# First batch's chains of pieces take turns between the attention's steps; last parts fetch operands during the experts of the chunk in front

## The chip, the cores and the metric

The kernel runs on one core of one Trainium2 chip. The metric is the device time of one execution in microseconds (us). A core has a matrix engine (TensorE, PE in the profile; PEld are its weight loads), a vector engine (DVE), an engine for functions such as exp (ACT), a general engine (POOL), and SP, which here only issues DMAs. Each engine takes its instructions strictly in the order in which the program gives them[...].

## The reference

The input x is 4 batches of 64 x 64 tokens with 128 channels, all float32. Two layers follow each other:

- Layer 0: elu(x), a 3x3 convolution 128 to 128, a second one 128 to 256 whose halves a and b give c3 = a * sigmoid(b); then a causal attention over the 4096 tokens of a batch with one query and key of 4 channels and a value of 16 channels, whose result goes through W3; x + c3 + that is the layer's output t.
- Layer 1: t = t + A(layernorm(t)), where A is an attention with 16 heads of 8 channels over all 4096 tokens, followed by its output product wo and a gated FFN of width 344 with a residual each; then t = t + M(layernorm(t)), where M routes each token to 2 of 8 experts (a 128 x 128 product and a bias each) and adds them with their gates.

In layer 1 the attention is the large part: per batch 16 heads x 4096 x 4096 exponentials.

## The kernel before, in words

A batch is cut into 8 chunks of 512 tokens. All work on layer 1's attention is done in **steps** (`attention_step`, line 820): one key tile of 128 tokens against one chunk of 512 queries for 4 heads. A step has four score matmuls on PE (`s<-qx,f_kx`), two exps of 128 x 1024 on ACT (`e<-s`), and four value matmuls on PE (`acc<-e,vg`), which `finish` (line 234) lets run two steps behind the scores. A batch has 8 chunks x 4 groups of 4 heads x 32 key tiles = 1024 steps, the kernel 4096.

`plan` (from line 1146) lists the steps as segments. A batch can only begin when its queries, keys and values exist. So the first batch goes in three turns: with the first 2 chunks alone (n = 2, 64 steps), then with 4 chunks (192 steps), then with all 8 (768 steps); partial sums go to DRAM (`d_p`). The other batches go in one turn of 1024 steps. A segment may start when `second` of its batch, the number of chunks whose operands are ready, has reached n.

Everything else is written as Python generators, "chains", each cut into **pieces** by `yield cost, word`: `convolutions` (line 439, Winograd products `m<-v,f_wino`, their sums on DVE and their row and column terms `r` and `v` on POOL), `first_attention` (line 576, layer 0's attention for a chunk, whose own steps go through `steps_in`), `second_operands` (line 650: product with W3, layernorm, transposition `m<-f_consts,h`, queries, values and keys of layer 1 for a chunk, stored to DRAM), and `last_part` (line 863: everything of a chunk after its attention, up to the output). "held" means that the piece has left its PSUM bank half written; "wait" and "rounds" that it has nothing to do until something else is done.

Before the first step, and after the last one, the chains run without steps (`alone[0]` is True): `run_alone` (line 1044) goes round all of them, and `bank` (line 162) hands out three PSUM buffers in turn. While steps run, `alone[0]` is False, and all chains share **one** PSUM bank, `m`. They stand in the list `fillers`; `insert` (line 245) takes one piece of the first one after a step. How often is set by `credit` and `rate` in the main loop (lines 1241 to 1267): one piece a step while the first batch is not ready, and later so many that the estimated rest is spread over the steps left. `quiet` keeps the first two steps of a segment free of pieces. While `stream` has no step to give, because `second` is too small, the loop counts as `waiting` and inserts one piece per turn.

In the first batch after line 1237 the list holds `second_operands_beside` (line 736), which returns at once when no chunk is ready, and `first_attention`. The latter does everything in one chain: if it lacks the convolution of its chunk it takes a piece of `st.conv` itself (line 583), then does the chunk's layer 0 attention, then runs `second_operands` for it (line 645), then takes the next chunk.

`last_part` loads its operands from DRAM (sums and values of the attention, h and t), stores the reciprocals of the sums, loads them again spread over the heads (`per`), and multiplies; eight pieces with no work on PE give the DMAs time. Further down, the experts' gates are turned by a store to DRAM (`d_g<-turned`) and four loads (`g<-d_g`), six empty pieces follow, then the product of the gates with the experts' biases (`tokens(ps, g8, eb, ...)`), then the experts' own products: for each of 4 token blocks two halves, which DVE multiplies by the gates (`by_e`), sums (`added`) and adds to t; then t is stored.

In the profile nearly all instructions carry line 105, since the class `InOrder` issues them all; groups are told apart by the names of their tiles.

Of the kernel before, what the change touches and what calls it, by code (L numbers as in the profile page):

```python
# [115 lines left out]
def fast_path(ctx: ExitStack, tc: tile.TileContext, a: dict, where: dict, out: bass.AP, verdict):  # L116
# [45 lines left out]
    def bank():  # L162
        return s_tile()[:, :QB] if alone[0] else m_tile()
# [275 lines left out]
    def convolutions(b, st):  # L439
# [88 lines left out]
        for n, (layer, r) in enumerate(jobs):  # L528
            ahead, terms = [], []
            at_once = False  # L530
            if n + 1 < len(jobs):
                layer_, r_next = jobs[n + 1]
                if layer_ == 0:
                    yield from elu(min(2 * r_next + 3, NQ))
                    if r_next == 3:
                        pool.memset(e_band[1][:, 17, :], 0.0)

                at_once = layer_ == 0 or layer == 1 or r_next + 1 < r
                if at_once:
                    terms.append(row_terms((c_band if layer_ else e_band)[r_next % 2]))  # L540

            def used(q):
                if at_once:
                    ahead.append(col_terms(terms[0], COLS[q]))

            if layer == 0:
                yield from winograd(wino1, slice(0, C), v, b1, used, first(r))
                here, above = c_band[r % 2], c_band[(r - 1) % 2]
                if r == 0:
                    pool.memset(here[:, 0, :], 0.0)  # L550
                else:
                    pool.tensor_copy(here[:, 0, :], above[:, 16, :])
                    pool.tensor_copy(above[:, 17, :], here[:, 1, :])
                if r == 3:
                    pool.memset(here[:, 17, :], 0.0)
            else:
                while alone[0] and len(st.ready) < 2 * r - 2:
                    yield 0.0, "wait"
                st.c3 = wk.tile([P, 2 * QB], FP, tag="c3", bufs=2, name="c3")
                yield from winograd(wino2, slice(0, C), v, half_b2a, lambda q: None, second(r, False))  # L560
                yield from winograd(wino2, slice(C, 2 * C), v, b2[:, 1:2], used, second(r, True))
                st.done += [st.c3[:, :QB], st.c3[:, QB:]]
                yield 0.0, "done"
            if n + 1 < len(jobs) and not at_once:
                terms.append(row_terms(c_band[r_next % 2]))
                ahead = [col_terms(terms[0], j) for j in COLS]
            v = ahead
# [8 lines left out]
    def first_attention(b, st):  # L576
        top0 = small("top0", [2, NQ])
        top_v0 = small("topv0", [NQ])
        xt = load_x(b, 0, "xt")
        for c in range(NQ):  # L580
            while len(st.done) <= c:

                yield (0.0, "wait") if alone[0] else next(st.conv, (0.0, "stop"))
            while alone[0] and st.second < c - 1:
                yield 0.0, "wait"
            c3 = st.done[c]
            t = xt
            pool.tensor_tensor(by_k(t), by_k(t), b3.unsqueeze(1).to_broadcast([P, 4, C]), ALU.add)
            if c + 1 < NQ:
                xt = load_x(b, c + 1, "xt")  # L590

            ps = bank()
            yield from halves(ps, wq0, c3)
            u, qx0 = chunk("u"), chunk("qx0")
            dve.tensor_scalar(u, ps, bq0, 0.25, ALU.add, ALU.mult)
            dve.tensor_reduce(top0[:, 0, c : c + 1], u, AX.X, ALU.max, apply_absolute_value=True)
            two_terms(u, qx0, "q")
            yield 0.46, "stop"
            ps = bank()
# [12 lines left out]
            u = chunk("u")[:, :P]  # L612
            dve.tensor_scalar(u, ps[:, :P], bk0, None, ALU.add)
            v0c = v0[:, 4 * c : 4 * c + 4, 1 : 1 + DV0]
            dve.tensor_tensor(
                v0c,
                few[:, :, :DV0],
                bv0.unsqueeze(1).to_broadcast([P, 4, DV0]),
                ALU.add,
            )  # L620
            dve.tensor_reduce(top0[:, 1, c : c + 1], u, AX.X, ALU.max, apply_absolute_value=True)
            dve.tensor_reduce(
                top_v0[:, c : c + 1],
                v0[:, 4 * c : 4 * c + 4, :].rearrange("p k s -> p (k s)"),
                AX.X,
                ALU.max,
                apply_absolute_value=True,
            )
            two_terms(u, kx0[:, c, :], "k")
            yield 0.24, "stop"  # L630

            ps = bank()
            transposed(c3, ps)
            dve.tensor_tensor(t, ps, t, ALU.add)
            yield 0.6, "stop"

            while alone[0] and st.read < c:
                yield 0.0, "wait"
            sums, found = [], []
            for r in range(c + 1):  # L640
                steps_in.append(first_step(c, r, qx0, sums, found))
            while not found:
                yield 0.0, "rounds"
            st.ready.append((t, found[0]))
            while not alone[0] and st.second <= c:
                yield from second_operands(b, st)
        dve.tensor_reduce(seen[:, 0, b : b + 1], top0.rearrange("p i c -> p (i c)"), AX.X, ALU.max)
        dve.tensor_reduce(seen[:, 1, b : b + 1], top_v0, AX.X, ALU.max)
# [87 lines left out]
    def second_operands_beside(b, st):  # L736

        while st.second < NQ:
            while len(st.ready) <= st.second or not folded[0]:
                if not alone[0]:  # L740
                    return
                yield 0.0, "wait"
            yield from second_operands(b, st)

# [75 lines left out]
    def attention_step(b, seg, kt, place, qx, vg, part):  # L820
# [19 lines left out]
        def values(es):  # L840
# [8 lines left out]
            if kt == seg.hi - 1:  # L849
# [5 lines left out]
                to = scratch[b]["a"][c, g] if seg.hi == NT else scratch[b]["p"][g, c]  # L855
                sp.dma_start(out=to, in_=at)
                if seg.hi == NT and g == NG1 - 1:
                    fillers.append([last_part(b, c), LAST])

        return scores, values  # L860


    def last_part(b, c):
        d = scratch[b]
        t, h, an = chunk("xt", "t"), chunk("xe", "h"), chunk("pos", "an")

# [4 lines left out]
        sp.dma_start(out=h, in_=d["h"][c])  # L871
        sp.dma_start(out=t, in_=d["t"][c])
        for _ in range(3):
            yield 0.0, "stop"
        dve.reciprocal(rs, rs)
        sp.dma_start(out=d["r"][c], in_=rs)
        per = chunk("pos", "per")
# [1 line left out]
            out=per, in_=d["r"][c].rearrange("(j i) n -> j (i n)", i=HD1).unsqueeze(1).to_broadcast([NH1, HD1, QB])  # L879
        )  # L880
        for _ in range(4):
            yield 0.0, "stop"
        dve.tensor_tensor(an, an, per, ALU.mult)
        yield 0.0, "stop"
        ps = bank()
        tokens(ps, an, wo1, range(2))
        yield 0.46, "held"
# [97 lines left out]
        by_block = d["g"][c].rearrange("(b e) (k a) -> b e k a", e=SLOT, a=SLOT)  # L985
        for b_ in range(4):
            sp.dma_start(out=g8.rearrange("e (k b a) -> b e k a", k=4, a=SLOT)[b_], in_=by_block[b_, :NE])
        for _ in range(6):
            yield 0.0, "stop"

        ps = bank()
        tokens(ps, g8, eb, range(2))
        yield 0.46, "held"
        tokens(ps, g8, eb, range(2, 4))
        dve.tensor_tensor(t, ps, t, ALU.add)
        yield 0.46, "stop"
        for k in range(4):
            tk = t[:, k * C : (k + 1) * C]
            by_e = wk.tile([P, NE, C], FP, tag="two", bufs=1, name="by_e")
            for half in range(2):  # L1000
# [8 lines left out]
                if half == 1:  # L1009
                    added = chunk("w", "added")[:, :C]  # L1010
                    dve.tensor_reduce(added, by_e.rearrange("p e c -> p c e"), AX.X, ALU.add)
                    dve.tensor_tensor(tk, tk, added, ALU.add)
                yield 0.46, "stop"
        sp.dma_start(out=tb_o[b][:, 4 * c : 4 * c + 4, :], in_=by_k(t))


# [23 lines left out]
            batches.append(self)  # L1040

    batches = []

    def run_alone(gens, until):

# [189 lines left out]
        lambda: st.second >= plan[0].n and len(spread_of) == 3,  # L1235
    )
    alone[0] = False

    fillers.extend([gen, PREPARE] for gen in reversed(left[1:]) if gen is not st.conv)

    steps = stream()
    credit, waiting = 0.0, False
    while True:
# [11 lines left out]
        b = now[0]  # L1255
        if batches[b].second == NQ and len(batches) == b + 1 and b + 1 < B:
            Batch(b + 1)
            fillers.append([first_attention(b + 1, batches[b + 1]), PREPARE])

        rate = 1.0  # L1260
        if batches[b].second == NQ:
            within = steps_left[b] - 40 if b + 1 < B else min(steps_left[b] - 40, 160)
            rate = sum(us for _, us in fillers) / max(1, within)
        credit = min(0.7, credit + rate)
        if waiting or credit > 0.0 and not quiet[0]:
            credit -= insert()
        finish(2)
    finish(0)
    alone[0] = True
# [718 lines left out]
```

## Time and profile before

| what | value |
|---|---|
| median of 3 runs | 8251.99 us (8248.94 to 8252.69) |
| profiled execution | 8255.66 us, its span 8253.9 us |
| mean granted PE clock | 0.983 |
| PE busy | 8031.3 us, 97% of the span |
| ACT busy | 7874.2 us, 95% |
| DVE busy | 2468.4 us, 30% |
| POOL busy | 680.1 us, 8% |
| exps of the steps, `e<-s` | 8480 instructions |
| first step of the attention of layer 1 | 149.5 us after the span's start |
| end of the last step's value matmuls | about 8171 us |

The profiled execution's own time is 1.8 us above its span and 3.7 us above the median of the runs. Busy times of PE are modelled, since matmuls overlap each other, so a PE that is busy all the time need not be at its limit. In the views below, a line of the timeline gives start, length, engine, operation, output<-input and count, and in brackets how long the engine was idle before and who ended that. A line of a table by windows gives the stretch, its length, then busy time and number of instructions of PE, PEld, DVE, ACT and POOL, the granted PE clock, the DMA share and GB/s. A line of the chain of waits gives start, length and what the end of the program was waiting for at that time. A line of the waits gives the total, the number and the longest, in us.

### The profile page before, as it was taken

Reading aid. Unit: us, or ns where it says so; the run is one execution under the profiler, and the core shown is the slowest. Engines: PE = TensorE matmul, PEld = TensorE weight load, DVE = VectorE, ACT = ScalarE, POOL = GpSimd, SP = SyncE. Lnnn points to the kernel's source line nnn. Section 1 sums busy time; section 2 is a strip of 40 time slices with the busy share of each in tenths; the row PEclk is TensorE's granted clock in tenths of the full one; section 3 lists DMA queues with packets and bytes.
Section 4 is the critical chain, followed back from the end, with each engine's and each line's share of the span. In section 5 each row is a group of like instructions: output and inputs, shape, how many; then the busy total and the mean of one; then the engine's idle time right before and its main releaser. Section 6 shows DMA issues by size and latency. Waiting matters only on the chain.

```text
span 8253.9 us, 172977 instructions
## 1 busy us (share of the span) xinstructions
PE 8031.3 (97%) x73299; PEld 2481.4 (30%) x73299; DVE 2468.4 (30%) x5068; ACT 7874.2 (95%) x8679; POOL 680.1 (8%) x615
## 2 busy tenths in 40 slices
PE   7799999999999999999999999999999999999997
PEld 3222222223333322333333333233333333332233
DVE  4433222222322223333322222343332222221223
ACT  3599999999999999999999999999999999999996
POOL 2210211000000003110000000311100000000000
PEclk8799999999999999999999999999999999999998
DMA  2121001101100001111100000111111111111211
GB/s 75 52 71 64 27 32 40 52 26 50 48 24 24 30 19 35 35 38 47 39 30 25 27 28 19 33 36 48 35 42 49 44 40 46 52 38 38 66 60 38
DMA packets 213940, 334.24 MB, mean 40 GB/s; under 512 B 31555, under 2 KB 107811, under 8 KB 213155
## 3 DMA queue, kind: packets, MB, share of 16 engines
q1 hardware_dynamic: 209139, 321.31, 11.9%
q8 instruction: 577, 9.45, 0.5%
q10 hardware_dynamic: 4016, 1.77, 0.1%
q14 instruction: 208, 1.70, 0.1%
HBM read 195.09 MB, written 127.93 MB: 39 GB/s over the span
## 4 chain that ended last, share of the span: by engine, by line
PE 87%; issue 7%; DVE 2%; ACT 1%; DMA 1%; POOL 1%; SPq 0%; ACTq 0%; DVEq 0%; POOLq 0%
PE acc L105 42%; PE s L105 29%; PE m L105 17%; ACT e L105 1%; DVE h L105 0%; POOL rs L105 0%; DMA f_kx<-d_k 0%; DVE pos L105 0%; DVE added L105 0%; DMA xe<-in_x_dram 0%; POOL xt L105 0%; DVE at L105 0%; SPq L105 0%; DMA d_r<-sums 0%; DVE two L105 0%
## 5 line engine op out<-in xcount | busy, mean ns | idle before, releaser
L105 ACT ACTIVATE e<-s 128x1024 f32<-128x1024 f32 (+1 forms) x8480 | 7814.2, 1101 | 144.5 <-PE s L105 137.9
L105 PE MATMUL acc<-e,vg 128*9 128x512 f32 x32768 | 4335.4, 595 | 1.0 <-DVE at L105 1.0
L105 PE MATMUL s<-qx,f_kx 32*128 32x512 f32 (+2 forms) x16960 | 2912.0, 496 | 40.3 <-ACT e L105 24.8
L105 PEld LDWEIGHTS s<-qx,f_kx 32*128 32x128 f32 (+1 forms) x16960 | 1165.5, 182 | 4089.1 <-ACT e L105 3872.2
L105 PEld LDWEIGHTS acc<-e,vg 128*9 128x9 f32 x32768 | 719.6, 90 | 798.0 <-issue 458.5
L105 PE MATMUL m<-v,f_wino 128*32 128x256 f32 x5744 | 468.1, 400 | 18.8 <-POOL v L105 7.3
L105 DVE TENSOR_TENSOR by_e<-m,gates 128x512 f32<-128x512 f32 x245 | 169.4, 691 | 681.6 <-PE m L105 681.6
L105 POOL TENSOR_TENSOR v<-r 128x1024 f32<-128x1024 f32 x120 | 232.6, 1945 | 1160.7 <-PE m L105 1160.3
L105 DVE COPY sd<-m 128x512 f32<-128x512 f32 x179 | 123.7, 691 | 633.5 <-PE m L105 633.5
L105 PE MATMUL m<-f_we,y2T 128*32 128x256 f32 x3920 | 313.1, 391 | 0.0
L105 POOL TENSOR_TENSOR rs<-ve,f_minus_half 128x4 f32<-128x4 f32 x64 | 65.3, 1020 | 2843.5 <-DVE ve L105 2819.8
L105 DVE TENSOR_REDUCE added<-by_e 128x128 f32<-128x1024 f32 x128 | 255.7, 1998 | 4.4
L105 DVE TENSOR_TENSOR t<-m,t 128x512 f32<-128x512 f32 x62 | 42.9, 692 | 698.7 <-PE m L105 698.7
L105 POOL TENSOR_TENSOR t<-t,h 128x512 f32<-128x512 f32 x32 | 40.9, 1277 | 2527.4 <-DVE h L105 2527.4
L105 DVE COPY at<-acc 128x512 f32<-128x512 f32 x130 | 89.9, 692 | 521.3 <-PE acc L105 521.3
L105 PE MATMUL m<-hT,f_fw 128*32 128x256 f32 (+1 forms) x2728 | 236.1, 391 | 0.0
L105 DVE TENSOR_TENSOR t<-m,sums 128x256 f32<-128x256 f32 x135 | 57.3, 424 | 480.1 <-PE m L105 480.1
L105 PEld LDWEIGHTS m<-v,f_wino 128*32 128x32 f32 x5744 | 116.4, 109 | 203.5 <-issue 155.0
L105 DVE SCALAR_TENSOR_TENSOR h<-m,h 128x512 f32<-128x512 f32 (+1 forms) x93 | 64.2, 690 | 352.6 <-ACT th L105 254.5
L105 DVE COPY h<-m 128x512 f32<-128x512 f32 (+1 forms) x93 | 64.2, 690 | 314.1 <-PE m L105 314.1
L105 PE MATMUL m<-e,f_v 128*32 128x512 f32 (+2 forms) x1128 | 154.0, 593 | 0.0
L105 DVE TENSOR_TENSOR e<-e,f_consts 128x128 f32<-128x128 f32 x128 | 29.1, 286 | 315.1 <-ACT e L105 315.1
(253 smaller groups left out, 3319.9 us busy)
## 6 DMA issues: line engine op xcount, KB each, us to landing
f_kx<-d_k SPq DMA_DIRECT2D x139, 512.0 KB
qx<-d_q SPq DMA_DIRECT2D x152, 256.0 KB
d_q<-two SPq DMA_DIRECT2D x64, 512.0 KB
d_a<-at SPq DMA_DIRECT2D x128, 256.0 KB
vg<-d_v SPq DMA_DIRECT2D x32, 576.0 KB
d_k<-two SPq DMA_DIRECT2D x32, 512.0 KB
d_v<-vc SPq DMA_DIRECT2D x32, 288.0 KB
xe<-in_x_dram SPq DMA_DIRECT2D x32, 256.0 KB
```

Of the source, the lines that this page charges most:

```text
L105: made = op(*args, **kw)
```

## The change

Two things are changed.

In the first batch the remaining chains are kept apart after line 1237 and put into one filler, `together`. It goes round them: one piece of a chain, then the next chain; it stays with a chain over "held" and "rounds", and passes over one that says "wait". For that the chains of batch 0 wait for each other by `b == 0` instead of `alone[0]`, so `first_attention` neither takes pieces of the convolution itself nor runs `second_operands`; `second_operands_beside` does that throughout. And as long as `second` of batch 0 is below 4, each turn of the main loop that inserts a piece inserts a second one.

In `last_part` the fetching of the operands is moved out into a generator `operands`. While the experts of a chunk run, each of their eight halves also takes one step of the `operands` of the last part that follows in the list, if there is one. The product of gates and biases is moved behind the experts, and the six empty pieces ahead of it are gone.

```diff
@@ convolutions, first_attention @@
-                while alone[0] and len(st.ready) < 2 * r - 2:
+                while b == 0 and len(st.ready) < 2 * r - 2:
...
-                yield (0.0, "wait") if alone[0] else next(st.conv, (0.0, "stop"))
-            while alone[0] and st.second < c - 1:
+                yield (0.0, "wait") if b == 0 else next(st.conv, (0.0, "stop"))
+            while b == 0 and st.second < c - 1:
...
-            while alone[0] and st.read < c:
+            while b == 0 and st.read < c:
...
-            while not alone[0] and st.second <= c:
+            while b > 0 and st.second <= c:
@@ second_operands_beside @@
-                if not alone[0]:
-                    return
@@ attention_step @@
-                    fillers.append([last_part(b, c), LAST])
+                    fillers.append([last_part(b, c), LAST, (b, c)])
@@ last_part @@
+    fetching, fetched = {}, {}
+
+    def operands(b, c):
...
+        dve.tensor_tensor(an, an, per, ALU.mult)
+        fetched[b, c] = t, h, an
+        yield
+
+    def fetch(b, c):
+
+        if (b, c) not in fetching:
+            fetching[b, c] = operands(b, c)
+        return next(fetching[b, c], fetching) is None
+
+    def fetch_following(b, c):
+        keys = [part[2] for part in fillers]
+        at = keys.index((b, c)) + 1
+        if at < len(keys) and keys[at]:
+            fetch(*keys[at])
+
+    def last_part(b, c):
+        d = scratch[b]
+        while fetch(b, c):
             yield 0.0, "stop"
-        dve.tensor_tensor(an, an, per, ALU.mult)
-        yield 0.0, "stop"
+        t, h, an = fetched.pop((b, c))
...
-        for _ in range(6):
-            yield 0.0, "stop"
-
-        ps = bank()
-        tokens(ps, g8, eb, range(2))
-        yield 0.46, "held"
-        tokens(ps, g8, eb, range(2, 4))
-        dve.tensor_tensor(t, ps, t, ALU.add)
-        yield 0.46, "stop"
         for k in range(4):
...
+                fetch_following(b, c)
                 yield 0.46, "stop"
+        ps = bank()
+        tokens(ps, g8, eb, range(2))
+        yield 0.46, "held"
+        tokens(ps, g8, eb, range(2, 4))
+        dve.tensor_tensor(t, ps, t, ALU.add)
+        yield 0.46, "stop"
@@ new @@
+    def together(gens):
+
+        gens = list(gens)
+        while gens:
+            for _ in range(len(gens)):
+                r = next(gens[0], None)
+                while r is not None and r[1] in ("held", "rounds"):
+                    yield r
+                    r = next(gens[0], None)
+                gen = gens.pop(0)
+                if r is not None:
+                    gens.append(gen)
+                    if r[0] > 0.0 or r[1] != "wait":
+                        yield r
+                        break
+                if not gens:
+                    return
+            else:
+                yield 0.0, "stop"
@@ main loop @@
-    fillers.extend([gen, PREPARE] for gen in reversed(left[1:]) if gen is not st.conv)
+    fillers.append([together(left), PREPARE, None])
...
             credit -= insert()
+            if b == 0 and batches[0].second < plan[0].n + 2:
+                insert()
```

More of the change, by code (lines that the diff above doesn't have):

```diff
@@ L857, in values @@
                 if seg.hi == NT and g == NG1 - 1:
-                    fillers.append([last_part(b, c), LAST])
+                    fillers.append([last_part(b, c), LAST, (b, c)])
         return scores, values
-    def last_part(b, c):
+    fetching, fetched = {}, {}
+    def operands(b, c):
         d = scratch[b]
@@ L881, in last_part @@
         for _ in range(4):
+            yield
+        dve.tensor_tensor(an, an, per, ALU.mult)
+        fetched[b, c] = t, h, an
+        yield
+    def fetch(b, c):
[10 more added lines that the diff above has]
+        while fetch(b, c):
             yield 0.0, "stop"
-        dve.tensor_tensor(an, an, per, ALU.mult)
-        yield 0.0, "stop"
+        t, h, an = fetched.pop((b, c))
         ps = bank()
@@ L987, in last_part @@
             sp.dma_start(out=g8.rearrange("e (k b a) -> b e k a", k=4, a=SLOT)[b_], in_=by_block[b_, :NE])
-        for _ in range(6):
-            yield 0.0, "stop"
-        ps = bank()
-        tokens(ps, g8, eb, range(2))
-        yield 0.46, "held"
-        tokens(ps, g8, eb, range(2, 4))
-        dve.tensor_tensor(t, ps, t, ALU.add)
-        yield 0.46, "stop"
         for k in range(4):
@@ L1257, in fast_path @@
             Batch(b + 1)
-            fillers.append([first_attention(b + 1, batches[b + 1]), PREPARE])
+            fillers.append([first_attention(b + 1, batches[b + 1]), PREPARE, None])
         rate = 1.0
@@ L1262, in fast_path @@
             within = steps_left[b] - 40 if b + 1 < B else min(steps_left[b] - 40, 160)
-            rate = sum(us for _, us in fillers) / max(1, within)
+            rate = sum(part[1] for part in fillers) / max(1, within)
         credit = min(0.7, credit + rate)
```

## The prediction, made before the changed kernel was run

> **What bounds the kernel now.** I began with the busy times and the forty slices of the page, to see where the two full engines are not full.
>
> ```profile
> PE 8031.3 (97%) x73299; PEld 2481.4 (30%) x73299; DVE 2468.4 (30%) x5068; ACT 7874.2 (95%) x8679; POOL 680.1 (8%) x615
> ...
> PE   7799999999999999999999999999999999999997
> ...
> ACT  3599999999999999999999999999999999999996
> ```
>
> ACT is full but for the first two slices and the last: exps set the pace, and only the two ends have anything to give. Next the busy times by window, cut at the turns of the first batch and at the last step:
>
> ```profile
> 149.50:273.60 124.10, 123.10 (x1148) 36.91 (x1152) 42.52 (x73) 118.54 (x129) 34.59 (x27) 0.95 0.15 44
> 273.60:374.50 100.90, 58.83 (x488) 22.17 (x480) 55.45 (x125) 13.13 (x16) 13.40 (x11) 0.55 0.21 71
> 374.50:795.70 421.20, 406.84 (x3744) 124.47 (x3746) 144.55 (x320) 402.26 (x440) 48.01 (x42) 0.97 0.17 57
> 795.70:815.70 20.00, 4.16 (x32) 2.12 (x26) 7.76 (x18) 1.85 (x4) 0.00 (x0) 0.60 0.64 201
> ...
> 8171.00:8178.40 7.40, 2.72 (x12) 2.06 (x12) 6.92 (x8) 0.00 (x0) 0.00 (x0) 0.83 0.09 35
> 8178.40:8254.00 75.60, 29.93 (x115) 23.32 (x115) 32.28 (x73) 2.12 (x4) 2.42 (x3) 0.61 0.08 24
> ```
>
> Row 1 is the turn with 2 chunks; row 2 the wait for chunks 2 and 3, with ACT busy for 13 us of 101; row 3 the turn with 4 chunks; row 4 the wait for chunk 7. Rows 5 and 6 follow the last step: the rest of chunk 6's experts, then all of chunk 7's last part. The timeline of PE then gives the prices, first a step with one piece, then the same pieces in row 2:
>
> ```profile
> 235.23 0.51 PE L105 MATMUL s<-qx,f_kx 32*128 32x512 f32 x4
> 235.67 0.64 PE L105 MATMUL m<-v,f_wino 128*32 128x256 f32 x8
> 236.12 1.04 PE L105 MATMUL acc<-e,vg 128*9 128x512 f32 x8
> 237.10 0.51 PE L105 MATMUL s<-qx,f_kx 32*128 32x512 f32 x4
> ...
> 277.28 1.87 PE L105 MATMUL m<-v,f_wino 128*32 128x256 f32 x16 [0.96 <-DVE t L105]
> 279.94 1.94 PE L105 MATMUL m<-v,f_wino 128*32 128x256 f32 x16 [0.79 <-DVE sd L105]
> 282.91 1.93 PE L105 MATMUL m<-v,f_wino 128*32 128x256 f32 x16 [1.03 <-DVE t L105]
> ```
>
> From start to start: scores 0.44, piece 0.45, values 0.98, so PE needs 1.42 us for a bare step and 1.87 with one piece. ACT does up to 223 exps per 200 us in its fullest stretches, 1.80 us a step. With one piece PE is just the slower. In the wait two pieces fill the one bank `m`, then DVE must empty it: (285.65 - 277.28)/3 = 2.79 us for each use of the bank. Last, the chain of waits and the waits at the end:
>
> ```profile
> 366.42 3.37 DMA d_k<-two
> 369.85 4.58 DMA f_kx<-d_k
> ...
> 8178.43 0.40 SPq L105
> 8178.91 2.31 DMA sums<-d_a
> ...
> 8220.68 2.23 DMA d_g<-turned
> ...
> 8227.23 5.76 PE s L105 x16
> ```
>
> ```profile
> PE s L105 <- DMA g<-d_g: 11.7, 1, 11.7
> ```
>
> Stored keys need 8 us until the next turn can begin. At the end, chunk 7's first load stands behind chunk 6's output on SP, and PE waits 11.7 us for the turned gates with the experts queued behind.
>
> **What the Trainium skill says.** "Perfetto Trace Analysis", section "Identifying the Most-Contended Engine", says that busy time of matmuls doesn't measure how near PE is to its limit. The trace agrees: PE is shown busy throughout a step that takes 1.87 us, and needs 1.42 of it when no piece is there. "TensorE: Matmul & The Clock Gate", "What's actually happening", says that PE falls to half its clock after a window of little activity. The trace agrees: 16 matmuls on `m` take 1.07 us at 275.25 and 1.94 at 279.94, and row 2 has a granted clock of 0.55. So I price the bank's use in a wait at 2.79 us. "DMA: Bandwidth & Descriptors", "Two DMAs through the same engine are not ordered", says that a DMA which reads what another wrote must be issued only after the first has landed; the trace shows it: `d_g` is issued at 8220.68, the first `g` at 8222.99.
>
> **The change, part by part.** Counts of pieces come from the order in which the two built programs stand.
>
> (1) *Start.* While the first keys load (PE waits until 149.53), the four waiting turns insert eight pieces instead of four. Two more uses of the bank from about 147.1 end near 152.6: **+3**.
>
> (2) *Turn with 2 chunks.* Before: 48 steps with a piece, 16 without: 48 x 1.87 + 16 x 1.80 = 118.6; measured 124.1, so 5.5 go to three slow steps at its start and a POOL wait. After: 37 steps carry two pieces. No double step is in the trace; PE's own work is 1.42 + 2 x 0.45 = 2.33 us. Below that it can't fall, PE being in order. Above: the next piece may only begin when DVE has emptied `m`, which took 0.94 to 1.15 us after the last matmul, and 1.42 us (values and next scores) lie between; so DVE's evacuation is hidden, and if it were not (a POOL or layernorm wait ahead of it), I bound it by +1 us a step. I take 2.33. Further 6 steps have one piece, 21 none, and chunks 2 and 3's seven steps of layer 0 (3 + 4), which before stood in row 2, now run here at 1.80: 37 x 2.33 + 6 x 1.87 + 28 x 1.80 = 147.8, plus the same 5.5, plus 3 for PE waiting at c3's gates (5.1 us before, at 292.7): 156.3 against 124.1, **+32**.
>
> (3) *Wait for chunks 2 and 3.* Before: 100.9. After, the built order has these uses of `m` between the 64th step and the next turn: for chunk 2 transposition, queries, values, keys (354.79 to 365.35 in the trace: 10.6 us), for chunk 3 the two products with W3 (3.7) and the same four (10.6): 24.9. Between them, by turns, 15.5 uses by the convolution for chunks 4 to 7: 15.5 x 2.79 = 43.2. That is the cost of taking turns: nothing in this turn needs them. Before, such pieces lay in steps that ACT bounds. Chunk 3's layernorm holds DVE for 4 (PE waited 4.5 at 354.79), and PE waits 7.3 for row and column terms on POOL (as at 408.66), now with chunk 2's products queued behind. The layernorm's `pow` stands ahead of those terms on POOL; the `vc` memset stands behind them, about when PE gets there: 0 to 2. The keys' 8 us lie beside the last 3.5 uses. Sum 79.4: **-22**.
>
> (4) *Turn with 4 chunks and the wait after it.* Before: 122 steps with a full piece and 96 others (26 of layer 0): 401, measured 421.2 (4 us of slow clock at the start, 10 at 401 to 412, 6 at 476 to 484), then 20.0 of waiting. After: 98 and 120, so 399; slow start 4 again, 6 for gates again, the POOL wait is now in (3). The eighth chunk is ready 44 steps before the turn's end, so row 4 goes. What comes late in its place is batch 1's first load of x, for which exp in `elu` waits on ACT ahead of the steps' exps; at 3117 and 5183 that cost about 4.5. Sum 413.6 against 441.2: **-28**.
>
> (5) *Steps from 815.7 to 8171.* Total pieces in steps stay within 1%, all under ACT. The fetch moves five loads, one store and two DVE operations per chunk earlier on SP and DVE; each gets at least two pieces' time (3.6 us) to land. If SP were held up by one, the next `qx` or `f_kx`, fetched a segment ahead, would still be in time. **0**, from -4 to +4.
>
> (6) *After the last step.* The last part of chunk 7 has none in front of it when it is queued, so its fetch is not early. But the fetches shorten the earlier ones: in the built order chunk 6 ends 38 steps before the last instead of after it. The load `sums<-d_a` then follows the store of `at` (issued at 8171.72) once that has landed, 2.2 (as `d_g`) to 3.4 (as `d_k`) later: 8174.5 instead of 8178.91, **-4.4**. And the experts no longer wait for `g`: DVE can begin at 8220.7 and needs 4 x 3.45 = 13.8 us (8235.7 to 8239.15 is one block), then 0.7 for the biases, whose gates land at 8227: t is complete at 8235.3 instead of 8246.2, **-10.9**. If DVE's cover were gone, PE would wait at the end as it does now.
>
> Sum: 3 + 32 - 22 - 28 + 0 - 15.3 = **-30**. The profiled execution, 8255.7, becomes 8225.4; it stands 3.7 above the median, so I forecast **8222 us**.
>
> **The rivals.** (a) *The first batch gains nothing.* For it: (1) to (3) already sum to +13, and only row 4 pays that back; one further stall a turn, each like the 5 to 9 us seen before, is enough. Against: row 4 goes by 44 steps of margin. Then only (6) remains: about 8237. (b) *The waits are cheaper.* With other chains between, PE's gaps may be too short for the slow clock; a use then costs 1.07 + 0.85 = 1.9 as at 275 to 277, and 26 uses save 0.85 each: 8200. For it: the slowdown came only after 4 us of gaps; against: 1.9 us with 1.07 busy still leaves PE idle for 0.8 of it. (c) *Double pieces choke on the single bank, and the kernel gets slower.* If DVE's evacuation is held behind sums, layernorm or POOL so that each of 37 double steps takes 3.3 us (+37) and each of 26 uses in the wait 3.5 (+19), the time is 8278. It decides from 1.42 us between matmul and empty bank; DVE is busy for 42.5 of 124 us in row 1, and 80 pieces instead of 48 bring that to some 57%, which speaks against. (d) *The change doesn't do what it says*: for chunk 7 the early fetch never happens; that is in (6) already.
>
> **How the numbers follow.** Forecast case 50%, its own range 8207 to 8237 (row (3) at 68 to 88, one stall more or less); (a) 24%; (b) 17%; (c) 9%. About 0.2%, 16.5 us, is what a measurement can tell from no change: faster is below 8235.5. From the forecast case 45 of 50, from (a) 10 of 24, (b) all: faster 0.71; same 0.21; slower 0.08. The range 8198 to 8249 leaves out half of (b)'s lower side, and (c).
>
> **What would show it.** Right: the first step of the 4-chunk turn comes later (near 388), with double steps of 2.33 us before it; ACT no longer idles near 800; from the last step's end to the last output 15 us less; no PE wait for `g`. Wrong: PE waits on DVE or POOL inside double steps; bank uses in the wait far from 2.8 us; exps slowed behind `neg<-xe`; or a changed pace of steps between 1000 and 8000.

## The result, and the profile after

| | before | after |
|---|---|---|
| median of 18 runs each | 8252.22 us (8246.71 to 8257.38) | 8236.88 us (8233.5 to 8242.52) |
| ratio, 95% interval | | 0.9982 (0.9975 to 0.9988) |
| profiled execution | 8255.66 us | 8237.05 us |

The change gains 15 us where 30 were forecast. The size is that of rival (a), but it isn't made up as (a) has it: the first batch loses 15 us, the steps after it gain 18 and the end 16. The page of the changed kernel, busy times and slices of PE and ACT:

```profile
PE 8026.9 (97%) x73335; PEld 2480.2 (30%) x73335; DVE 2459.3 (30%) x5068; ACT 7869.3 (96%) x8679; POOL 680.3 (8%) x615
...
PE   6799999999999999999999999999999999999998
...
ACT  2499999999999999999999999999999999999996
```

Work and its amount are as before. The first two slices of ACT were 3 and 5 tenths full and are now 2 and 4: the first batch got emptier, not fuller. The table by windows of the changed kernel, cut at the same events as the one of before (turn with 2 chunks, wait, turn with 4 chunks, the steps after it, what follows the last step):

```profile
154.90:334.00 179.10, 152.36 (x1504) 48.67 (x1504) 80.95 (x166) 134.68 (x145) 46.85 (x37) 0.97 0.12 37
334.00:417.70 83.70, 47.19 (x440) 17.97 (x432) 47.69 (x88) 0.63 (x1) 30.08 (x24) 0.54 0.21 74
417.70:831.20 413.50, 403.57 (x3532) 122.49 (x3536) 135.48 (x308) 403.17 (x445) 42.62 (x35) 0.98 0.21 68
831.20:8168.50 7337.30, 7295.63 (x67392) 2219.51 (x67384) 2081.29 (x4268) 7313.09 (x8064) 511.40 (x451) 1.00 0.12 38
8168.50:8235.20 66.70, 29.99 (x115) 22.76 (x115) 32.84 (x74) 2.12 (x4) 2.41 (x3) 0.65 0.09 27
```

Against the ledger: the start is at 154.9 instead of 149.5; the turn with 2 chunks takes 179.1 (forecast 156.3, before 124.1); the wait 83.7 (forecast 79.4, before 100.9); the turn with 4 chunks 413.5 with no wait behind it (forecast 413.6, before 441.2); the steps after it 7337 (before 7355, forecast no change); the end 66.7 (before 82.9). Two rows are far off: the turn with 2 chunks, and the steps after the first batch.

What a double step looks like there is in PE's timeline of the changed kernel, first near 162, then where it turns over, then near 211:

```profile
162.27 0.51 PE L105 MATMUL s<-qx,f_kx 32*128 32x512 f32 x4
162.71 1.07 PE L105 MATMUL m<-v,f_wino 128*32 128x256 f32 x16
163.60 1.04 PE L105 MATMUL acc<-e,vg 128*9 128x512 f32 x8
164.57 0.51 PE L105 MATMUL s<-qx,f_kx 32*128 32x512 f32 x4
165.01 1.07 PE L105 MATMUL m<-v,f_wino 128*32 128x256 f32 x16
...
188.27 0.66 PE L105 MATMUL m<-f_consts,pos 128*128 128x128 f32 x4 [1.95 <-DVE pos L105]
192.50 1.08 PE L105 MATMUL m<-v,f_wino 128*32 128x256 f32 x8 [3.58 <-POOL v L105]
...
211.53 0.64 PE L105 MATMUL m<-v,f_wino 128*32 128x256 f32 x8
213.14 0.64 PE L105 MATMUL m<-v,f_wino 128*32 128x256 f32 x8 [0.97 <-DVE t L105]
213.57 1.07 PE L105 MATMUL acc<-e,vg 128*9 128x512 f32 x8
214.56 0.50 PE L105 MATMUL s<-qx,f_kx 32*128 32x512 f32 x4
215.00 0.64 PE L105 MATMUL m<-v,f_wino 128*32 128x256 f32 x8
216.45 0.64 PE L105 MATMUL m<-v,f_wino 128*32 128x256 f32 x8 [0.81 <-DVE sd L105]
```

At 162 the step's two pieces stand in one group of 16 matmuls, both halves of one use of the bank `m`, and the period is 165.01 - 162.71 = 2.30 us: the forecast's 2.33. At 188.27 comes a piece that fills the bank by itself (a transposition), and after it the pairs are shifted by one: at 211.53 the first piece is the second half of one use, the next one the first half of another. Now PE must wait inside the step until DVE has emptied the bank (0.97, 0.81), and the period is 215.00 - 211.53 = 3.47. From the starts of the exps, of the steps in this turn 11 take 2.32 us in the mean and 19 take 3.33; 14 of the 19 stand in three groups between 204.9 and 259.7, and a few of the others wait for something else. Two steps more are slow, for another reason: the step with the transposition takes 9.03 us and the next one 5.18. The second piece of the first needs the terms `v` that POOL is still making (3.58 us of waiting at 192.50), and what stands behind it is slow too (the next eight value matmuls take 1.93 us instead of 1.04). The timeline of ACT shows these steps from the other side, 0.43 us without an exp in a step whose pieces share one use, 7.09 behind the wait for POOL, and 1.53 in a shifted step:

```profile
165.17 1.94 ACT L105 ACTIVATE e<-s 128x1024 f32<-128x1024 f32 x2 [0.43 <-PE s L105]
...
196.11 1.94 ACT L105 ACTIVATE e<-s 128x1024 f32<-128x1024 f32 x2 [7.09 <-PE s L105]
...
215.17 1.94 ACT L105 ACTIVATE e<-s 128x1024 f32<-128x1024 f32 x2 [1.53 <-PE s L105]
```

The end is as predicted. The chain of waits of the changed kernel after the last step:

```profile
8169.19 1.99 DMA d_a<-at
8171.20 2.10 DMA sums<-d_a
...
8212.65 1.51 DMA d_g<-turned
8214.26 1.90 DVE added L105
```

The load of the sums follows the store of `at` directly, and the experts' sums on DVE begin beside the store of the gates; no wait for `g` is left in the chain.

So the theory: a double step costs 2.3 us when its pieces share one use of the bank, and 3.3 when they straddle two; this is what ate the gain of the first batch, and the edits to the last part carry the whole gain. The rivals: two pieces a step are too much for DVE or POOL at that place, however paired; or the gain in the steps after 831 belongs to the turns.

### The profile page after: what moved, and what is told of

It is laid out like the page before. It is cut to its first block, busy times and chain, and to the rows that moved or that the text cites. A ratio compares the mean times of both kernels' runs of the same rounds, so it can differ in the third digit from the quotient of the medians.

```text
span 8235.2 us, 173069 instructions
## 1 busy us (share of the span) xinstructions
PE 8026.9 (97%) x73335; PEld 2480.2 (30%) x73335; DVE 2459.3 (30%) x5068; ACT 7869.3 (96%) x8679; POOL 680.3 (8%) x615
## 4 chain that ended last, share of the span: by engine, by line
PE 88%; issue 7%; DVE 2%; ACT 2%; POOL 1%; DMA 0%; ACTq 0%; SPq 0%; DVEq 0%; POOLq 0%
PE acc L105 42%; PE s L105 29%; PE m L105 18%; ACT e L105 1%; DVE h L105 0%; DVE t L105 0%; POOL rs L105 0%; DVE two L105 0%; DVE sd L105 0%; DVE top L105 0%; POOL xt L105 0%; POOL v L105 0%; DVE at L105 0%; DVE pos L105 0%; POOL r L105 0%
## 5 line engine op out<-in xcount | busy, mean ns | idle before, releaser
L105 ACT ACTIVATE e<-s 128x1024 f32<-128x1024 f32 x8480 | 7813.5, 1113 | 98.1 <-PE s L105 93.9
L105 PE MATMUL s<-qx,f_kx 32*128 32x512 f32 (+1 forms) x16960 | 2910.5, 495 | 38.3 <-ACT e L105 28.3
```

The source lines that it names most:

```text
L105: made = op(*args, **kw)
```

## The experiments

Each kernel was run with several repetitions beside the kernel before, whose own median lay between 8252.2 and 8257.5; each ratio is to the one beside it, and medians of different rows can be compared only to some 5 us. The parts below are cut from each profiled execution by the number of the exp (of 8480): to the first exp of the turn with 4 chunks, that turn with the wait behind it, the steps after it, and what follows the last exp.

| kernel | median, us | ratio to before (95%) | to turn 4 | turn 4 | steps after | end |
|---|---|---|---|---|---|---|
| before | 8252.2 | 1 | 375.5 | 440.2 | 7354.2 | 84.1 |
| the change | 8236.9 | 0.9982 (0.9975 to 0.9988) | 418.6 | 412.5 | 7336.2 | 67.9 |
| last parts alone | 8222.4 | 0.9969 (0.9956 to 0.9981) | 369.2 | 439.9 | 7343.1 | 67.8 |
| turns alone | 8268.4 | 1.0019 (1.0011 to 1.0027) | 417.4 | 412.0 | 7352.3 | 83.5 |
| no second piece | 8253.6 | 1.0002 (0.9993 to 1.0010) | 434.7 | 412.7 | 7336.1 | 67.8 |
| pairs aligned | 8214.8 | 0.9955 (0.9941 to 0.9969) | 394.6 | 414.5 | 7336.0 | 68.0 |
| pairs straddled | 8260.8 | 1.0003 (0.9995 to 1.0012) | 434.6 | 412.9 | 7344.1 | 68.3 |
| biases moved alone | 8228.8 | 0.9970 (0.9959 to 0.9981) | 371.3 | 439.9 | 7347.2 | 68.0 |
| early fetch alone | 8332.3 | 1.0088 (1.0075 to 1.0102) | 373.8 | 437.7 | 7441.5 | 79.0 |
| operands first | 8206.7 | 0.9942 (0.9929 to 0.9956) | 368.8 | 428.4 | 7339.3 | 68.3 |
| operands first, aligned | 8185.3 | 0.9918 (0.9904 to 0.9931) | 349.0 | 427.8 | 7340.8 | 67.6 |
| the same through turn 4 | 8217.0 | 0.9955 (0.9941 to 0.9968) | 363.0 | 449.1 | 7338.0 | 67.0 |

**Halves of the change.** The last parts' edits alone: the first batch's chains as before (`alone[0]` again, no `together`, no second piece).

```diff
-    fillers.append([together(left), PREPARE, None])
+    fillers.extend([gen, PREPARE, None] for gen in reversed(left[1:]) if gen is not st.conv)
...
-            if b == 0 and batches[0].second < plan[0].n + 2:
-                insert()
```

> The early fetch and the moved biases alone; the first batch is treated as in the kernel before. Theory (my ledger with step (5) corrected): the end gives its 16 us (82.9 to 66.8 after the last step), whatever the first batch does, so about 8236 against the 8252 before, and the first batch's turns are worth nothing net. If the 18 us that the steps from 816 to 8171 also lost come from the earlier fetches (fewer stalls at the batches' ends), it is lower than that, 8218 to 8230. Rival: the 18 us come from the turns (chains of batch 1 start at another place): then 8236 exactly and the start and first 816 us as before.

And the turns alone, with `last_part` as before:

```diff
-        while fetch(b, c):
-            yield 0.0, "stop"
-        t, h, an = fetched.pop((b, c))
...
-                fetch_following(b, c)
```

> The first batch's chains by turns and the second piece per step alone; the last parts fetch and add their biases as before. Theory that the first batch as a whole loses: start +5, turn with two chunks +55, wait -17, turn with four chunks -28 and the 20 us wait behind it inside that: +15, so 8267 if nothing in the later steps changes. Rival: the 18 us of the later steps come with the turns: about 8250, no change. The end after the last step stays at about 83 us in both.

Measured: 8222.4 and 8268.4. Beside the 8252.8 of these runs' kernel before, the first gains 30.4 and the second loses 15.6; the sum, -14.8, is the change's -15.3. The halves add up, and the turns are a loss by themselves. Of the 18 us by which the steps after 816 got shorter, 11 come with the last parts' edits and 2 with the turns alone; the other 5 are within what executions differ by (below).

**One piece or two.** The change without the second piece per step.

```diff
-            if b == 0 and batches[0].second < plan[0].n + 2:
-                insert()
```

> The change without the second piece per step (one piece in each step of the turn with two chunks). Theory (double steps are dear because of the one bank): the turn with two chunks falls back from 179 to about 137 us (64 steps at 1.80 to 1.87 and the seven first ones of layer 0), while the wait for chunks 2 and 3 then holds 99 pieces, some 47 uses of the bank at 2.75, so about 130 instead of 84: together +4, 8241. Rival (pieces are dear wherever they stand, but steps hide none of a second piece): the wait grows by less than the turn shrinks, 8215 to 8225.

Measured: 8253.6, 17 us slower than the change, which neither side had expected. Its windows, the turn with 2 chunks and the wait:

```profile
151.90:272.60 120.70, 119.71 (x1136) 35.80 (x1137) 41.86 (x73) 118.53 (x129) 34.49 (x27) 0.97 0.15 45
272.60:434.70 162.10, 97.04 (x840) 35.86 (x838) 89.70 (x183) 13.77 (x18) 45.40 (x35) 0.57 0.14 46
```

The turn shrinks to 120.7 (the seven layer 0 steps, which I had counted here, stay in the wait: 13.77 us on ACT), but the wait, at a granted clock of 0.57, takes 162: 78 us more, where the turn saves 58. Two pieces in a wait cost about 2.8 us, a use of the bank; a straddled pair makes a step only 1.5 us longer (3.33 instead of 1.80). With chains by turns, the second piece is needed.

**How the pair lies.** The second piece only if the first one left the bank half written, and the opposite.

```diff
+        held[0] = r is not None and r[1] == "held"
...
-            if b == 0 and batches[0].second < plan[0].n + 2:
+            if b == 0 and batches[0].second < plan[0].n + 2 and held[0]:
```

> The change, with one condition more: a step takes a second piece only if its first one left the bank half written, so a pair is always both halves of one use of the bank. Theory (parity): a double step that holds one use costs 2.3 us, one that holds the second half of a use and the first half of the next costs 3.4, since PE then waits inside the step for the bank to be emptied. With all 38 double steps aligned the turn with two chunks takes 150 to 160 us instead of 179, with 1 to 5 back in the wait: 8213 to 8222, about 8217. Rival (what costs is the sum of work on VectorE and GpSimd behind two pieces, or the slower clock, not how they pair): the turn stays at 175 or more and the time within 5 us of the change's 8237.

```diff
-            if b == 0 and batches[0].second < plan[0].n + 2:
+            if b == 0 and batches[0].second < plan[0].n + 2 and not held[0]:
```

> The opposite of the aligned pairs: a step takes a second piece only if its first one has closed a use of the bank, so every pair holds the second half of one use and the first half of the next. Theory (parity): the 3.33 us that the change's 19 such steps took now hold for all its double steps, 30 to 38 of them, where the aligned kernel has 24 at 2.30: the turn with two chunks at 180 to 195 us against 178 in the change and 154 with aligned pairs; 8237 to 8255. Rival (what made the 19 steps slow was their place in the turn, for instance what VectorE or GpSimd did then): a turn of about 178 again and no steps at 3.3 before 188 us.

Aligned: 8214.8, 22 us less than the change, all of it before the turn with 4 chunks (394.6 against 418.6; the start differs by 3.6 between these two executions). Windows of that kernel, the turn with 2 chunks and the wait:

```profile
152.20:306.00 153.80, 147.64 (x1472) 49.62 (x1476) 80.11 (x160) 134.33 (x145) 46.10 (x36) 0.97 0.14 44
306.00:394.60 88.60, 50.34 (x476) 19.30 (x468) 49.77 (x94) 0.68 (x3) 30.09 (x24) 0.55 0.20 70
```

These windows run from the first exp of the turn to the end of its last, and on to the next turn's first exp; cut so, the change's turn is 177.8 us and its wait 85.1. So the turn is 24 us shorter, with nearly the same busy time on DVE (80.1 against 80.95), POOL and ACT, and the wait grows by 3. In its PE timeline, at the places where the change had the transposition and where it straddled:

```profile
186.39 0.66 PE L105 MATMUL m<-f_consts,pos 128*128 128x128 f32 x4
...
191.89 1.07 PE L105 MATMUL m<-v,f_wino 128*32 128x256 f32 x16
...
217.27 1.07 PE L105 MATMUL m<-v,f_wino 128*32 128x256 f32 x16
218.16 1.04 PE L105 MATMUL acc<-e,vg 128*9 128x512 f32 x8
219.13 0.51 PE L105 MATMUL s<-qx,f_kx 32*128 32x512 f32 x4
219.57 1.07 PE L105 MATMUL m<-v,f_wino 128*32 128x256 f32 x16
```

219.57 - 217.27 = 2.30; 24 steps of this turn take 2.30, one 3.17. Step by step beside the change, the 24 us have two parts. The 14 steps in three groups that straddled take 33.0 us instead of 47.5: 14.5 less. And the two steps from the transposition on take 3.7 instead of 14.2: 10.5 less. What is left, 1 us, goes the other way. A transposition leaves nothing half written, so it gets no second piece here, and the product that needs `v` comes only at 191.89, without a wait for POOL. The condition removes both costs at once.

Straddled: 8260.8, with 8257.5 for the kernel before beside it. The turn takes 195.0 us (151.7 to 346.7) and has 31 steps at 3.37. PE's timeline of the straddled kernel:

```profile
261.71 0.64 PE L105 MATMUL m<-v,f_wino 128*32 128x256 f32 x8
263.16 0.64 PE L105 MATMUL m<-v,f_wino 128*32 128x256 f32 x8 [0.81 <-DVE sd L105]
263.62 1.04 PE L105 MATMUL acc<-e,vg 128*9 128x512 f32 x8
264.59 0.51 PE L105 MATMUL s<-qx,f_kx 32*128 32x512 f32 x4
265.03 0.64 PE L105 MATMUL m<-v,f_wino 128*32 128x256 f32 x8
266.70 0.64 PE L105 MATMUL m<-v,f_wino 128*32 128x256 f32 x8 [1.03 <-DVE t L105]
```

265.03 - 261.71 = 3.32, and steps of 3.3 to 3.6 us begin early in the turn (169.8, 173.1, 176.7), where the change's took 2.30. So what makes a step take 3.3 us is the pairing, not the place or the load on DVE: the change's turn (19 such steps) lies between the two. The wait for POOL is there too: the two steps in question take 10.9 us. The steps after the turn with 4 chunks, 7344.1, are 8 us above the change's, though the edit doesn't touch those steps; so the split of the 18 us is no finer than that.

**The two edits of the last part.** The biases' product moved, without the early fetch; then the early fetch, with the biases where they were.

```diff
-                fetch_following(b, c)
```

> The biases' product moved behind the experts, without the early fetch; the first batch as in the kernel before. Theory (step (6) as two separate gains): the end gives the 10.9 us of the experts that no longer wait for the gates, while the 4.4 us of the load behind the store, and the 11 us that the early fetch took out of the steps from 816 on, stay away: about 8242, with about 72 us after the last step. Rival (what shortened the steps is the shorter last part, not the fetch): 8231. If the load's place on SP was no cost, the end is 67 us as with the fetch.

```diff
+        for _ in range(6):
+            yield 0.0, "stop"
+
+        ps = bank()
+        tokens(ps, g8, eb, range(2))
+        yield 0.46, "held"
+        tokens(ps, g8, eb, range(2, 4))
+        dve.tensor_tensor(t, ps, t, ALU.add)
+        yield 0.46, "stop"
         for k in range(4):
...
-        ps = bank()
-        tokens(ps, g8, eb, range(2))
-        yield 0.46, "held"
-        tokens(ps, g8, eb, range(2, 4))
-        dve.tensor_tensor(t, ps, t, ALU.add)
-        yield 0.46, "stop"
```

> The early fetch alone: the biases' product stands ahead of the experts, with its six empty rounds, as in the kernel before; the first batch too is as before. Theory (the predicted split of step (6), as far as the move of the biases alone has left it standing): the experts wait for the gates again, so the end keeps 10.9 of its 16 us and is 78 to 79 us; the steps from 816 on gain the 4 to 11 us that came with the fetch: about 8240. Rival (the fetch does nothing by itself, and the whole gain is the move of the biases): 8252, with 83 us at the end.

The biases alone: 8228.8, with the whole gain at the end (68.0). My theory had left 4.4 us of it to the fetch; six empty rounds less in each last part do as much for chunk 6: as in the change, the load of the sums follows the store of `at` as soon as that has landed (8160.24 and 8162.26 in its chain of waits). Between this and both edits (8222.4) the intervals overlap, so it isn't settled whether the fetch adds anything.

The early fetch alone: 8332.3, 75 us slower than the kernel before, which I had at 8240. Its end is 79.0, as the split of step (6) said; but the steps after the first batch are 87 us longer. The waits of this kernel from 850 to 8160, and its timeline at one of the places:

```profile
PE m L105 <- DVE an L105: 56.4, 27, 2.5
```

```profile
6320.58 1.91 DVE L105 TENSOR_REDUCE added<-by_e 128x128 f32<-128x1024 f32 x1
6322.53 0.29 DVE L105 TENSOR_TENSOR t<-t,added 128x128 f32<-128x128 f32 x1
6322.74 0.68 DVE L105 TENSOR_TENSOR an<-an,per 128x512 f32<-128x512 f32 x1
...
6323.57 0.64 PE L105 MATMUL m<-f_wo,an 128*32 128x128 f32 x16 [2.48 <-DVE an L105]
...
6326.47 1.94 ACT L105 ACTIVATE e<-s 128x1024 f32<-128x1024 f32 x2 [3.35 <-PE s L105]
```

The fetched operand `an` is finished on DVE behind the last expert's sum; the next last part's first product needs it at once, PE waits in order with the next scores behind it, and ACT stands still for 3.35 us. Of the 27 waits 21 are of 2.5 us; four steps around each of these take 2.5 to 4.3 us more than four of 1.85, some 79 of the 87 together. In the change the biases' product lies between the last expert and that product, and the waits of PE hold none for `an`. The biases behind the experts are the cover of the early fetch; it isn't worth having without them.

**Which chain goes first.** `together` doesn't go round: operands first, then layer 0, then the convolution, and a piece that costs PE nothing takes no place of its own any more; alone, with aligned pairs, and with aligned pairs until all 8 chunks are ready.

```diff
-        gens = list(gens)
+        gens = list(reversed(gens))
         while gens:
-            for _ in range(len(gens)):
-                r = next(gens[0], None)
+            for gen in list(gens):
+                r = next(gen, None)
...
-                gen = gens.pop(0)
-                if r is not None:
-                    gens.append(gen)
-                    if r[0] > 0.0 or r[1] != "wait":
-                        yield r
-                        break
+                if r is None:
+                    gens.remove(gen)
+                elif r[0] > 0.0:
+                    yield r
+                    break
```

> The change, but the waiting chains don't take turns: at each place the chain that makes the next operands goes first, then layer 0, and the convolution of the later chunks gets only the places that those leave. Theory (the wait for chunks 2 and 3 is long because the convolution's 15.5 uses of the bank stand between): after the 64 steps only 9 places are left, some 7 uses at 2.75 and the keys' 8 us with a wait or two for terms and layernorm, 30 to 45 us instead of 85; its 42 double steps are not aligned, so the turn with two chunks stays at 165 to 185; the turn with four at about 415: 8190 to 8205. Rival (the chain for chunks 2 and 3 is bound by its own latencies, which then hold up PE, in order, inside the steps): the turn with two chunks grows by as much as the wait shrinks, 8230 or more.

> Both: the next operands' chain first, and a second piece only as the other half of one use of the bank (34 double steps). Theory: turn with two chunks 155 to 165 (2.3 us a double step), then 18 places, some 14 uses at 2.75 and the keys' 8 us, 45 to 55 us; together about 205 to 215 instead of 242 with the aligned pairs alone, so 8178 to 8190, the fastest so far. Rival (latencies of the one chain move into the steps): no better than the aligned pairs alone, 8210 or more.

> As the one with both, but aligned second pieces go on through the turn with four chunks (47 double steps more), where no wait follows that they could shorten. Theory: that turn gets longer by what the order gives, 422.6 against 402.5 us of the larger of PE's and ScalarE's work, and the steps behind it have as many pieces fewer at 0.05 us each: 10 to 20 us slower than without. Rival (the earlier convolution of the later chunks, or fewer pieces in batch 1's steps, pays it back): the same within 5 us.

Operands first: 8206.7, just above what was expected. Cut by the exps as above, the wait falls from 85.1 to 23.0 us, but the turn before it grows from 177.8 to 190.6, with 20 steps at 3.34, five at 5.5 and the one of 9.0: the rival holds in part. With aligned pairs, the fastest kernel here, 8185.3, 68 us below the kernel before (8253.6 beside it) and 52 below the change. Its windows, the turn with 2 chunks (from 1.7 us ahead of its first exp), the wait, the turn with 4:

```profile
152.20:302.10 149.90, 142.59 (x1407) 47.26 (x1400) 73.49 (x149) 133.88 (x145) 45.41 (x35) 0.99 0.14 44
302.10:349.00 46.90, 26.19 (x280) 10.79 (x276) 28.05 (x59) 0.00 (x0) 3.77 (x5) 0.60 0.38 131
349.00:776.80 427.80, 408.04 (x3700) 124.85 (x3703) 150.33 (x337) 404.86 (x445) 58.25 (x48) 0.97 0.20 65
```

The wait is 47 instead of 89. Turn and wait together are 47 us shorter than with aligned pairs alone, and 49 shorter than the change's where the pairs aren't aligned, near the 43 that I had priced for the convolution's pieces in the wait; 13 us come back in the turn with 4 chunks, which gets those pieces (x337 on DVE instead of x308). The edit changes two things, the order and what takes a place, and no run separates them.

Second pieces through that turn too: 8217.0, 32 slower. The turn grows by 21 (20 were forecast), the steps after it gain 3, and what stands before the turn is 14 longer: 2 are the start, and 12 the wait. PE's timeline at the end of that wait:

```profile
360.27 1.94 PE L105 MATMUL m<-v,f_wino 128*32 128x256 f32 x16 [8.63 <-POOL v L105]
362.13 0.80 PE L105 MATMUL s<-qx,f_kx 32*128 32x512 f32 x4
```

Two and a half uses of the bank by the convolution now stand ahead of the turn's first scores; in the kernel with aligned pairs in the first turn alone the scores stand ahead of them, and start at 348.14. The last use waits 8.63 us for POOL, and the scores wait behind it, since PE takes them in order.

## Why the prediction was right or wrong

**(1) Start**: forecast +3, measured +5.4, of which 2.2 were there before the first changed instruction.

**(2) Turn with 2 chunks**: forecast +32, measured +55. This is the step that failed, at its price: "so DVE's evacuation is hidden [...] I take 2.33". The 1.42 us of values and scores lie between one use of the bank and the next only when a step's pair is one use. When it straddles, nothing lies between, and PE waits the full emptying: 1.0 us a step, 14.5 us in the three groups of 14 steps. The bound of +1 us a step had that size, but named another reason, a wait for POOL or a layernorm ahead of it. That wait came too, once, and cost 10.5 us, far above the bound. Together these 25 us, set against the aligned kernel, make up the 23 missed, the aligned kernel's turn being 2.5 below the forecast. That this turn, 153.8, comes near the 156.3 is in part luck: it has 24 steps at 2.30 where I had counted 37 double steps, so other terms must have been too small.

**(3) Wait**: forecast -22, measured -17. The mechanism is right: the turn-taking puts the convolution's pieces into the wait, and with operands first turn and wait together lose 47 to 49 us, where I had these pieces at 43.

**(4) Turn with 4 chunks**: 413.6 forecast, 413.5 measured; the wait of 20 us is gone.

**(5) Steps after it**: forecast 0, measured -18 in this pair of executions, 11 with the last parts alone. What disappears is seen in the waits of ACT between 850 and 8160, here before, then after:

```profile
ACT e L105 <- PE s L105: 25.0, 17, 3.2
ACT neg L105 <- issue: 1.5, 1, 1.5
...
ACT neg L105 <- DMA xt<-in_x_dram: 1.2, 1, 1.2
```

```profile
ACT e L105 <- PE s L105: 19.0, 14, 2.7
```

ACT no longer waits at a new batch's `neg` (1.2 us for x, and 1.5 for which the profile shows no other engine) and waits 6 us less for scores; the rest is spread thin (steps of 2.0 to 2.2 us: 95 before, 54 after). With the biases moved alone there are 57 such steps and with the turns alone 101, so this part goes with the moved biases. Shorter last parts leave the next batch's chain more room; I counted their pieces' work, which is unchanged, and not the rounds that they occupy. That this is the cause is argued, not shown.

**(6) End**: -15.3 forecast, -16 measured. The sum is right, its split isn't: the moved biases alone give all of it (-16), and the early fetch alone the part for the earlier load (-5), which either edit brings.

The forecast of 8222 thus missed by 15: +2, +23 and +5 in the first batch, -18 and -1 after it, and the rest is how the profiled execution stands to the median. That it missed by no more is luck: the 18 us of the later steps, which I had at nothing, cover most of the 30 that the first batch missed. Rival (a) met the size by the same luck: it had the first batch at nothing, which lost 15, and nothing in the later steps; its reason, "one further stall a turn", fits the one wait for POOL but not the straddled steps.

The Trainium skill, "Perfetto Trace Analysis", section "Optimization Strategy", says that the same gap repeating on the engine that should be full can mean that there isn't room in a memory for the next tile. The traces agree: ACT's gap of 1.4 to 1.6 us in each straddled step is the one PSUM bank, and 0.4 when the pair fits it. It is a sentence to apply to a step that a change will make, not only to gaps already seen.

## What to carry to other kernels

When two pieces of work per step share one buffer, price the step for each way in which the pair can lie across a use of the buffer, and make the schedule keep the cheap way; one odd piece is enough to shift all that follow. Two pieces of one chain in a row also leave less time to an engine that has work to do between them. Chains that take turns treat unequal urgencies as equal: in a stretch that ends with a wait, let the chain that the wait is for go first. An early fetch needs its consumer to come late as well: look at what lies between its last operation and its first use.

## What the runs showed of the hardware

A single wait of PE of 2.5 us can slow what comes next. In the kernel with the early fetch alone PE waits 21 times for 2.5 us. After the 2.48 us at 6323.57 eight value matmuls took 1.65 us and four score matmuls 0.80, where the same took 1.04 and 0.51 before it. After 17 of the 21 waits the eight value matmuls took 1.11 to 2.01 us; after the other four, 1.07. "TensorE: Matmul & The Clock Gate", section "What's actually happening", speaks of the lower clock after little activity; these waits agree, but for the four. I had read the trace of before as needing some 4 us of gaps; in fact its slow group at 277.28 comes after two gaps of 0.98 and 0.96 us.
